# A four-layer graph network: the last three destination chunks of layer 3 summed over lists of fetched rows in place of dense products

## The chip, the cores and the metric

The kernel runs on one core of a Trainium2 chip. The metric is the device time of one execution in microseconds (us). TensorE (PE) multiplies matrices; VectorE (DVE), ScalarE (ACT) and GpSimd (POOL) do the rest of the arithmetic; GpSimd and SyncE (SP) also issue DMA transfers.

## The reference

Each of four layers replaces x by layernorm(x + layer(x, adj)). `adj` is a 2708 x 2708 symmetric matrix of zeros and ones with about 16 ones in a row; x has 512 columns.

```python
def _layernorm(x, axis=-1, eps=1e-5):
    m = jnp.mean(x, axis=axis, keepdims=True)
    v = jnp.var(x, axis=axis, keepdims=True)
    return (x - m) / jnp.sqrt(v + eps)
deg = jnp.maximum((adj != 0).astype(jnp.float32).sum(-1), 1.0)
# layer 0: dinv = rsqrt(deg); relu(((dinv * (adj + I) * dinv) @ x + x) @ W0 + b0)
# layer 1: ((dis[:, None] * adj * dis[None, :]) @ x) @ W1.T + b1, dis = (adj.sum(1) + 1e-8) ** -0.5
# layer 2: twice: proj = x @ W; Wh, Ws = split(proj); a = softmax(Wh @ Ws.T) * adj
#          x = leaky_relu(a @ Wh + x, 0.01)
# layer 3: adj @ (x @ W3) + b3   (8 heads side by side)
```

For layer 3 the kernel computes (adj @ x) @ W3 + b3, then adds x and normalises.

## The kernel before

**Tiles and stages.** The 2708 nodes are 22 blocks of 128 rows (the last has 20). Where a layer sums over neighbours, the *destinations* are cut into six chunks of columns (`CH`): 512, 512, 512, 512, 384 and 276. The *sources* are taken in six groups of blocks (`GROUPS`: 0-3, 4-7, 8-11, 12-15, 16-18, 19-21). A step of the dense form is one pair (chunk k, group g).

**Dense sums (layers 0, 1 and 3).** `prepare` (L782) casts the mask bytes `at` to 32-bit tiles `m` on ScalarE, and, at a layer's first chunk, `halve` (L713) splits the rows x of a source block into two halves: `xh` by ScalarE and `xl` = x - `xh` by VectorE. `multiply` (L849) then adds into four accumulators `acc[k][d]`, one for each 128 of the 512 columns of x, the products `xh` x `m` and `xl` x `m` for every source block. After the last group `evict` (L919) moves the accumulators to `ht`, `project` (L936) multiplies each block of 128 destinations by W (four fp32 products `mm`), `combine` (L976) adds the residual row `xres`, and `finish` (L995) calls `layernorm` (L634) and writes the rows out. `residual` (L964) fetches `xres` by a DMA that GpSimd issues. Block 21 has only 20 rows: its projection is spread over four partitions' quarters (`few`, L652), and the four parts are then added (`total`, L662).

**The masks in DRAM.** While layer 0 runs, the bytes of `adj` are kept in DRAM tiles `masks[k]` (128 x 22 x width of the chunk), which layers 1 to 3 read again as `at<-mask`, loads that SyncE issues.

**Lists.** During layer 1, `index` (L1097) and `one_hot` (L1221) build, for every destination block, lists of 128 row numbers (`givers`): four "rest" lists of sources that any of the block's 128 destinations may have as a neighbour, and eight quarter lists, two for each 32 destinations (block 21: three lists only). Every neighbour of the block is in one of its lists once.

**Attention (layer 2).** Class `Attention` (L1275) works through two graph attention layers. For each destination chunk it computes scores and softmax weights, writes rows of `pairs` (a projected row of 512 numbers with weights at either side) to DRAM, fetches 128 of these rows for one list by an indirect DMA on GpSimd (`fetch`, L1562, into one of eleven buffers `wide`), and adds to an accumulator with one fp32 product for a full list, whose stationary operand is the fetched weights (128 x 128) and whose moving operand is the fetched row, or with four products of 128 x 32 for one turn of quarter lists (`weigh`, L1609). The rows after the second attention layer are kept on chip for the next layer, and written to `saved[2]` in DRAM.

**What sets the order.** `Ordered` (L53) chains the instructions of every engine in the order in which the program issues them, so each engine's queue is in program order and every issue is recorded at L70; groups of instructions are told apart by their tiles' names. The program itself decides the order by a clock of estimated costs: `advance` moves it, `later` puts off a step until it has passed, and generators that yield are taken as fillers. At the end of layer 2 the filler is `early` (L598): layer 3's products for chunks 0 to 2 (`TWO` = 3) and groups 0 to 3, since the rows of these sources are ready first. Their partial sums are copied to pages `begun`. After the attention, `step` (L1043) does the remaining steps: groups 4 and 5 of chunks 0 to 2, then all six groups of chunks 3, 4 and 5, with the projections and layernorms of a chunk done by `ends` (L1079) between the steps of the next.

## Time and profile before

| | us |
|---|---|
| median of 3 runs (2367.58 to 2376.91) | 2368.28 |
| the profiled execution, its own time | 2338.2 |
| span of the profile | 2336.5 |
| PE busy | 2274.8 |
| DVE busy | 1474.8 |
| ACT busy | 662.2 |
| POOL busy | 762.3 |

The mean granted TensorE clock is 0.993 of full speed. The profiled execution is 30 us shorter than the median of the runs. In the profile a row such as "PE acc<-m,xh 128*128 128x512 f32 x1" names the engine, the output and input tiles, the size of the stationary operand and that of the output; a bracket at its end gives the idle time before it and what ended it. "PEld" is the loading of stationary operands. An entry of the chain of waits has its start, its duration, the engine and the output tile. In a table of stretches each column is an engine's busy time, then the granted clock, the share of the DMA engines and GB/s.

### The profile page before, as it was taken

Reading aid. Unit: us, or ns where it says so; the run is one execution under the profiler, and the core shown is the slowest. Engines: PE = TensorE matmul, PEld = TensorE weight load, DVE = VectorE, ACT = ScalarE, POOL = GpSimd, SP = SyncE. Lnnn points to the kernel's source line nnn. Section 1 sums busy time; section 2 is a strip of 40 time slices with the busy share of each in tenths; the row PEclk is TensorE's granted clock in tenths of the full one; section 3 lists DMA queues with packets and bytes.
Section 4 is the critical chain, followed back from the end, with each engine's and each line's share of the span. In section 5 each row is a group of like instructions: output and inputs, shape, how many; then the busy total and the mean of one; then the engine's idle time right before and its main releaser. Section 6 shows DMA issues by size and latency. Waiting matters only on the chain.

```text
span 2336.5 us, 26171 instructions
## 1 busy us (share of the span) xinstructions
PE 2274.8 (97%) x8518; PEld 1292.5 (55%) x8518; DVE 1474.8 (63%) x2831; ACT 662.2 (28%) x1334; POOL 762.3 (33%) x879
## 2 busy tenths in 40 slices
PE   8999999999999999999999999999999999999997
PEld 6677677778644444443456444444443456566585
DVE  6999986786655529657677511228677788724523
ACT  6544353223100113222223200113232334432211
POOL 6645641111000000636375550000636466551000
PEclk9999999999999999999999999999999999999998
DMA  9765652222434404869699996405869799983311
GB/s 343 258 199 169 182 172 86 74 86 70 171 146 167 154 0 143 278 229 311 204 324 350 302 388 232 152 0 163 279 217 314 233 316 329 305 279 96 123 48 43
DMA packets 312440, 463.50 MB, mean 198 GB/s; under 512 B 60162, under 2 KB 189706, under 8 KB 312292
## 3 DMA queue, kind: packets, MB, share of 16 engines
q1 hardware_dynamic: 252276, 240.81, 31.5%
q0 software_dynamic: 60016, 220.92, 27.1%
q8 instruction: 69, 1.13, 0.2%
q14 instruction: 79, 0.65, 0.1%
HBM read 307.75 MB, written 153.85 MB: 198 GB/s over the span
## 4 chain that ended last, share of the span: by engine, by line
PE 84%; DVE 7%; DMA 4%; issue 2%; ACT 1%; POOL 1%; SPq 0%; DVEq 0%; ACTq 0%; POOLq 0%
PE sp L70 32%; PE acc L70 29%; PE mm L70 9%; PE z L70 6%; PE wst L70 6%; DMA pairs<-s 1%; DMA at<-in_adj_t 1%; DVE st L70 1%; DMA at<-mask 1%; ACT m L70 1%; DVE s L70 1%; PE list L70 1%; PE mix L70 0%; POOL bytes L70 0%; PE tr_x2t L70 0%
## 5 line engine op out<-in xcount | busy, mean ns | idle before, releaser
L70 POOL DMA_INDIRECT g<-pairs,givers x510 | 516.2, 1012 | 897.0 <-DMA pairs<-s 537.4
L70 PE MATMUL sp<-xs,wst_sb 128*128 128x512 f32 (+3 forms) x2112 | 797.7, 544 | 0.0
L70 PEld LDWEIGHTS sp<-xs,wst_sb 128*128 128x128 f32 (+1 forms) x2112 | 380.0, 186 | 406.8 <-issue 321.9
L70 PE MATMUL acc<-m,xh 128*128 128x512 f32 (+4 forms) x1584 | 571.4, 382 | 13.6 <-ACT m L70 7.0
L70 PE MATMUL acc<-m,xl 128*128 128x512 f32 (+4 forms) x1584 | 553.2, 367 | 1.5 <-DVE xl L70 1.5
L70 PEld LDWEIGHTS acc<-m,xh 128*128 128x128 f32 (+1 forms) x1584 | 290.3, 189 | 81.4 <-issue 22.3
L70 PEld LDWEIGHTS acc<-m,xl 128*128 128x128 f32 (+1 forms) x1584 | 290.3, 189 | 48.1 <-issue 5.7
L70 ACT COPY s<-sp 128x512 f32<-128x512 f32 (+2 forms) x252 | 133.6, 531 | 482.1 <-PE sp L70 469.5
L70 PE MATMUL acc<-g 128*32 128x512 f32 (+1 forms) x1020 | 260.8, 605 | 0.9 <-DMA g<-pairs,givers 0.5
L70 DVE TENSOR_TENSOR top<-top,s 128x512 f32<-128x512 f32 (+5 forms) x240 | 149.6, 623 | 170.6 <-ACT s L70 169.1
L70 PE MATMUL mm<-w,ht 128*128 128x512 f32 (+1 forms) x528 | 222.6, 593 | 8.1 <-DVE ht L70 8.1
L70 ACT CAST m<-at 128x512 fp32r<-128x512 uint8 (+5 forms) x396 | 199.2, 567 | 80.0 <-DMA at<-mask 63.7
L70 ACT ACTIVATE s<-s 128x512 f32<-128x512 f32 (+3 forms) x264 | 150.7, 580 | 236.6 <-DVE s L70 236.3
L70 DVE TENSOR_TENSOR sum<-sum,s 128x512 f32<-128x512 f32 (+4 forms) x252 | 157.4, 625 | 23.9 <-ACT s L70 23.9
L70 DVE TENSOR_TENSOR s<-s,a 128x512 f32<-128x512 f32 (+3 forms) x264 | 165.9, 628 | 10.2 <-DMA a<-mask 1.2
L70 DVE TENSOR_TENSOR s<-s,shift 128x512 f32<-128x512 f32 (+3 forms) x264 | 162.8, 620 | 6.7 <-ACT shift L70 6.7
L70 PEld LDWEIGHTS mm<-w,ht 128*128 128x128 f32 (+1 forms) x528 | 95.5, 186 | 124.4 <-issue 110.9
L70 PE MATMUL wst<-xt,mixed 128*128 128x512 f32 (+2 forms) x384 | 152.5, 550 | 1.7 <-ACT mixed L70 1.7
L70 PEld LDWEIGHTS acc<-g 128*32 128x32 f32 (+1 forms) x1020 | 75.4, 134 | 136.9 <-issue 115.8
L70 PE MATMUL z<-w,xt 128*128 128x512 f32 (+1 forms) x352 | 151.0, 596 | 0.0
L70 DVE COPY z_sb<-z 128x512 f32<-128x512 f32 (+1 forms) x44 | 30.3, 690 | 179.5 <-PE z L70 176.3
L70 POOL DMA_DIRECT2D x<-o x44 | 26.0, 596 | 358.0 <-DVE o L70 354.2
(167 smaller groups left out, 1657.4 us busy)
## 6 DMA issues: line engine op xcount, KB each, us to landing
pairs<-s SPq DMA_DIRECT2D x378, 128.0 KB
pairs<-z_sb SPq DMA_DIRECT2D x84, 512.0 KB
at<-in_adj_t SPq DMA_DIRECT2D x84, 256.0 KB
xres<-x POOLq DMA_DIRECT2D x44, 256.0 KB, 4.3
x<-o POOLq DMA_DIRECT2D x43, 256.0 KB, 3.1
x<-x SPq DMA_DIRECT2D x37, 256.0 KB
at<-mask SPq DMA_DIRECT2D x32, 256.0 KB
xt<-t SPq DMA_DIRECT2D x32, 256.0 KB
```

The lines of the kernel that those rows point to most:

```text
L70: ins = call(*args, **kw)
```

## The change

Layer 3's chunks 3, 4 and 5 (destination blocks 12 to 21) no longer have dense products. Each destination block is summed over its lists instead, as in the attention, then turned, projected and normalised.

- *Rows with bytes at their sides.* A new DRAM tile `rows3` has one row of 3220 bytes for each node: 640 bytes of `adj` for blocks 12 to 16, the 2048 bytes of x, 532 bytes of `adj` for blocks 17 to 21. The rows of x that the attention writes (`saved[2]`) now go to its middle. `give`, called in layer 1 after the eviction of chunks 3, 4 and 5, copies the bytes there from `masks[k]`, DRAM to DRAM, in four copies that SyncE issues (512 bytes a piece for chunk 3, 128 and 256 for chunk 4, 276 for chunk 5; 2816 pieces each).
- *Lists.* The new class `Listed` gathers the rows (one indirect DMA a list on GpSimd, 111 in all; a row brings the bytes of its block and what lies between them and x), casts the bytes of its block to fp32 weights on ScalarE (one cast of 128 x 128 for a full list, four of 128 x 32 for a quarter turn; three buffers in turn, which used to be the `hit` and `both` buffers of the lists' building), and multiplies. Block 21 comes first, then 12 to 20. After a block's last list VectorE copies the sum to `sum3`, TensorE transposes it in four pieces, ScalarE copies these to `turned3`, and the projection follows. Two blocks are normalised together.
- *The layernorm of `Listed`* does its last step on ScalarE (`scalar=True`: Identity with a scale and a bias), with one more small step on VectorE for the bias.
- *Order.* Group 4 of chunk 2 moves to the end of `early`, into the attention. The rest of chunks 0 to 2, in half steps, and their projections (`rest`) are the fillers between the lists. They use one half of PSUM, the lists the other.
- *Smaller things.* The residual rows of layer 3 are loaded by SyncE instead of GpSimd. Block 21's four parts are added straight to its residual. The `wide` buffers grow from 640 to 672 fp32 columns. The `hit` tile has one buffer in place of two.

The diff, without unchanged surroundings and with the old body of the projection loop left out:

```diff
@@ -41,6 +41,12 @@
+LISTED = (3, 4, 5)
+FIRST, MIDDLE = 12, 17
+ASIDE = (MIDDLE - FIRST) * P
+ROW = 4 * D
@@ -118,8 +124,13 @@
-            for s in range(3)
+            for s in range(2)
+        self.rows3 = scratch.tile(
+            [NP, ASIDE + ROW + N - MIDDLE * P], U8, tag="rows3", name="rows3"
+        )
+        x = self.rows3[:, ASIDE : ASIDE + ROW].bitcast(FP)
+        self.saved.append([x[i * P : (i + 1) * P, :] for i in range(NB)])
@@ -523,7 +534,7 @@
-    def wide(self, name, shape=(P, D + P)):
+    def wide(self, name, shape=(P, D + ASIDE // 4)):
         return self.wides.tile(list(shape), FP, tag="wide", name=name)
@@ -556,18 +567,14 @@
-            run.seq += [(l3, k, g) for g in (4, 5) for k in range(2)]
-            run.seq += [(l3, k, g) for k in range(2, TWO) for g in (4, 5)]
-            run.seq += [(l3, k, g) for k in range(TWO, len(CH)) for g in range(len(GROUPS))]
+            run.seq.append((l3, TWO - 1, 4))
+            run.early = len(run.seq)
+            run.seq += [(l3, k, g) for k in range(TWO) for g in (4, 5) if g == 5 or k < TWO - 1]
-            for t in range(4 * TWO, len(run.seq)):
-                self.step(run, t)
-            ly, k = run.before
-            for i, n, ps in self.project(ly, k):
-                self.finish(ly, k, [(i, n, self.combine(ly, i, n, ps))])
+            listed = Listed(self, l3)
+            listed.run(self.rest(run, listed))
@@ -604,7 +611,7 @@
         yield True
-        for t in range(4 * TWO):
+        for t in range(run.early):
             ly, k, g = seq[t]
@@ -616,22 +623,47 @@
-            if g == 3:
+            last = g == (4 if k == TWO - 1 else 3)
+            if last:
-            for n, j in enumerate(range(*GROUPS[g])):
+            for n in range(DC):
-                    self.multiply(ly, k, g, [j])
+                    self.multiply(ly, k, g, [n])
-                if g == 3:
+                if last:
-    def layernorm(self, rows):
+    def rest(self, run, listed):
+        for t in range(run.early, len(run.seq)):
+            ly, k, g = run.seq[t]
+            self.before_products(run, t)
+            if (ly, k) != run.before:
+                self.residual(ly, k)
+                run.before = ly, k
+            for d in range(DC):
+                self.multiply(ly, k, g, ds=[d])
+                listed.advance(3 * 2 * 0.226)
+                if d % 2:
+                    yield True
+            if g == 4:
+                continue
+            self.evict(ly, k)
+            self.biased(ly, k)
+            yield True
+            for i, n, ps in self.project_blocks(ly, k):
+                listed.advance(DC * cost(D))
+                listed.later(2.0, lambda a=(i, n, ps): listed.end(*a))
+                yield True
+    def layernorm(self, rows, scalar=False):
@@ -644,6 +676,18 @@
+        if scalar:
+            shift = small.tile([P, DC], FP, tag="ln_shift", name="ln_shift")[:, :m]
+            nc.vector.scalar_tensor_tensor(shift, mv[:, :m, 0], -1.0, y, ALU.mult, ALU.mult)
+            for q, (r, o, n) in enumerate(rows):
+                nc.scalar.activation(
+                    o[:n],
+                    r[:n],
+                    AF.Identity,
+                    bias=shift[:n, q : q + 1],
+                    scale=y[:n, q : q + 1],
+                )
+            return
@@ -850,26 +894,28 @@
-        starts, stops = ((0, 16), (15, NB - 2)) if two else ((0,), (NB - 2,))
+        b = GROUPS[4 if k == TWO - 1 else 3][1]
+        starts, stops = ((0, b), (b - 1, NB - 2)) if two else ((0,), (NB - 2,))
-            half = 0 if two and blocks[0] == 0 else k
+            half = 0 if two else k
-            for x in (ly.hi, ly.lo):
+            for x in (ly.hi, ly.lo) if 0 in ds else ():
-                        start=False,
+                        start=(blocks[0] in starts and x is ly.hi),
+            starts = ()
@@ -935,37 +981,31 @@
...
+    def project_blocks(self, ly, k):
+        half = 0 if ly.number == 3 else k
...
         for i, lo, n in blocks_of(k):
+            yield i, n, self.times_w(ly, half, i, n, lambda c: ly.ht[k][c][:, lo : lo + n])
+    def times_w(self, ly, half, i, n, columns):
+        nc, name = self.nc, f"mm{ly.number}_{i}"
+        if n <= QW:
+            return self.few(half, name, n, D, columns, lambda c: ly.w[c])
+        ps = self.bank(half, name)
+        for c in range(DC):
+            nc.tensor.matmul(ps[:n], columns(c), ly.w[c], start=(c == 0), stop=(c == DC - 1))
+        return ps
-            t = self.page(f"xres{ly.number}_{i}")
-            self.nc.gpsimd.dma_start(t, ly.source[i])
-            ly.done["xres", i] = t
+            self.residual_of(ly, i)
+    def residual_of(self, ly, i):
+        t = self.page(f"xres{ly.number}_{i}")
+        (self.nc.sync if ly.number == 3 else self.nc.gpsimd).dma_start(t, ly.source[i])
+        ly.done["xres", i] = t
@@ -976,6 +1016,10 @@
         nc, x = self.nc, ly.done.pop(("xres", i))
+        if n <= QW and ly.number == 3:
+            for c in range(DC):
+                nc.vector.tensor_add(x[:n], x[:n], ps[c * QW : c * QW + n])
+            return x
         if n <= QW:
@@ -992,7 +1036,7 @@
-    def finish(self, ly, k, parts):
+    def finish(self, ly, k, parts, scalar=False):
@@ -1000,7 +1044,7 @@
             out.append((i, o, n))
-        self.layernorm([(x, o, n) for (_, n, x), (_, o, _) in zip(parts, out)])
+        self.layernorm([(x, o, n) for (_, n, x), (_, o, _) in zip(parts, out)], scalar)
         for i, o, n in out:
@@ -1072,6 +1116,8 @@
             run.before, run.phase = (ly, k), 0
+            if ly.number == 1 and k in LISTED:
+                self.attention.give(k)
             if ly.number == 1:
@@ -1231,8 +1277,10 @@
-        tile_ = lambda tag, w: self.lists.tile([P, NB, w], BF, tag=tag, name=f"{tag}{s}", bufs=2)
-        hit, both = tile_("hit", LISTS), tile_("both", 2 * LISTS)
+        tile_ = lambda tag, w, bufs: self.lists.tile(
+            [P, NB, w], BF, tag=tag, name=f"{tag}{s}", bufs=bufs
+        )
+        hit, both = tile_("hit", LISTS, 1), tile_("both", 2 * LISTS, 2)
@@ -1311,6 +1359,19 @@
+    def give(self, k):
+        for i0, i1 in ((FIRST, MIDDLE), (MIDDLE, NB)):
+            blocks = [b for b in blocks_of(k) if i0 <= b[0] < i1]
+            if not blocks:
+                continue
+            lo, width = blocks[0][1], sum(n for _, _, n in blocks)
+            at = (blocks[0][0] - i0) * P + (ASIDE + ROW if i0 == MIDDLE else 0)
+            self.nc.sync.dma_start(
+                self.k.rows3[:, at : at + width].rearrange("(j p) i -> p j i", p=P),
+                self.k.masks[k][:, :, lo : lo + width],
+            )
@@ -1778,6 +1839,140 @@
+class Listed:
+    AHEAD = WIDES - 1
+    def __init__(self, fast, ly):
+        self.f, self.k, self.nc, self.ly = fast, fast.k, fast.nc, ly
+        blocks = [b for k in LISTED for b in blocks_of(k)]
+        self.to_weigh = []
+        for i, _, n in [blocks[-1], *blocks[:-1]]:
+            ts = lists_of(i)
+            self.to_weigh += [(i, n, t, t is ts[0], t is ts[-1]) for t in ts]
+        self.to_fetch = [(i, t) for i, _, ts, _, _ in self.to_weigh for t in ts]
+        self.fetched, self.pending = [], []
+        self.clock, self.free = 0.0, 3.0
+        self.done, self.turns = [], 0
+    def advance(self, us):
+        self.clock += us
+        while self.pending and self.pending[0][0] <= self.clock:
+            self.pending.pop(0)[1]()
+    def later(self, us, what):
+        self.pending.append((self.clock + us, what))
+        self.pending.sort(key=lambda a: a[0])
+    def fetch_ahead(self):
+        while self.to_fetch and len(self.fetched) < self.AHEAD:
+            i, t = self.to_fetch.pop(0)
+            g = self.f.wide(f"g3_{i}_{t}")
+            if i < MIDDLE:
+                first, width = (i - FIRST) * P, (MIDDLE - i) * P + ROW
+            else:
+                first, width = ASIDE, ROW + (i - MIDDLE) * P + rows_of(i)
+            self.nc.gpsimd.indirect_dma_start(
+                out=g.bitcast(U8)[:, :width],
+                out_offset=None,
+                in_=self.k.rows3,
+                in_offset=bass.IndirectOffsetOnAxis(ap=self.k.givers[:, i, t : t + 1], axis=0),
+                element_offset=first,
+            )
+            self.free = max(self.free, self.clock) + 1.25
+            self.fetched.append((g, self.free + 5))
+    def weigh(self, wait=False):
+        nc, f = self.nc, self.f
+        self.fetch_ahead()
+        if not self.to_weigh:
+            return False
+        i, n, ts, first, last = self.to_weigh[0]
+        there = self.fetched[len(ts) - 1][1]
+        if there > self.clock:
+            if not wait:
+                return False
+            self.advance(there - self.clock)
+        self.to_weigh.pop(0)
+        gs = [self.fetched.pop(0)[0] for _ in ts]
+        if first:
+            self.acc = f.bank(1, f"acc3_{i}")
+            f.residual_of(self.ly, i)
+        side = len(ts) > 1
+        self.turns += 1
+        tag, bufs = ("both", 2) if self.turns % 3 else ("hit", 1)
+        weights = f.lists.tile([P, P], FP, tag=tag, name=f"weights3_{i}", bufs=bufs)
+        at, z = (0, (MIDDLE - i) * P // 4) if i < MIDDLE else (ROW + (i - MIDDLE) * P, 0)
+        for h, g in enumerate(gs):
+            lo, rows = (h * QW, QW) if side else (0, n)
+            nc.scalar.copy(
+                weights[:, lo : lo + rows], g.bitcast(U8)[:, at + lo : at + lo + rows]
+            )
+        for h, g in enumerate(gs):
+            lo, rows = (h * QW, QW) if side else (0, n)
+            nc.tensor.matmul(
+                self.acc[lo : lo + rows],
+                weights[:, lo : lo + rows],
+                g[:, z : z + D],
+                start=first,
+                stop=last,
+            )
+        self.advance(1.1 if side else cost(D))
+        if last:
+            self.later(1.5, lambda a=(i, n, self.acc): self.turn(*a))
+        self.fetch_ahead()
+        return True
+    def turn(self, i, n, acc):
+        nc, f = self.nc, self.f
+        r = f.page(f"sum3_{i}")
+        nc.vector.tensor_copy(r[:n], acc[:n])
+        def turn():
+            ps = f.bank(1, f"tr3_{i}", (P, DC, P))
+            for c in range(DC):
+                nc.tensor.transpose(
+                    ps[:, c, :n], r[:n, bass.ts(c, P)], self.k.ident[:n, :n]
+                )
+            t = f.page(f"turned3_{i}", FP, (P, DC, P))
+            nc.scalar.copy(t[:, :, :n], ps[:, :, :n])
+            self.advance(0.45)
+            self.later(1.2, lambda: self.project(i, n, t))
+        self.later(1.2, turn)
+    def project(self, i, n, t):
+        f, x = self.f, self.ly.done["xres", i]
+        ps = f.times_w(self.ly, 1, i, n, lambda c: t[:, c, :n])
+        self.nc.vector.tensor_add(x[:n], x[:n], self.ly.bt[:n])
+        self.advance((1 if n <= QW else DC) * cost(D))
+        self.later(2.0, lambda: self.end(i, n, ps))
+    def end(self, i, n, ps):
+        f = self.f
+        self.done.append((i, n, f.combine(self.ly, i, n, ps)))
+        if len(self.done) > 1 or not self.to_weigh:
+            f.finish(self.ly, None, self.done, True)
+            self.done = []
+    def run(self, products):
+        while True:
+            if self.weigh() or next(products, False):
+                continue
+            if self.pending:
+                self.advance(self.pending[0][0] - self.clock)
+            elif not self.weigh(True):
+                return
```

More of the change, by code (lines that the diff above doesn't have):

```diff
@@ L936, in project @@
     def project(self, ly, k):
-        nc = self.nc
-        parts = []
+        return list(self.project_blocks(ly, k))
+    def project_blocks(self, ly, k):
+        half = 0 if ly.number == 3 else k
         for i, lo, n in blocks_of(k):
-            if n <= QW:
-                ps = self.few(
-                    k,
-                    f"mm{ly.number}_{i}",
-                    n,
-                    D,
-                    lambda c: ly.ht[k][c][:, lo : lo + n],
-                    lambda c: ly.w[c],
-                )
-                parts.append((i, n, ps))
-                continue
-            ps = self.bank(k, f"mm{ly.number}_{i}")
-            for c in range(DC):
-                nc.tensor.matmul(
-                    ps[:n],
-                    ly.ht[k][c][:, lo : lo + n],
-                    ly.w[c],
-                    start=(c == 0),
-                    stop=(c == DC - 1),
-                )
-            parts.append((i, n, ps))
-        return parts
+            yield i, n, self.times_w(ly, half, i, n, lambda c: ly.ht[k][c][:, lo : lo + n])
[7 more added lines that the diff above has]
+        return ps
     def residual(self, ly, k):
         for i, _, _ in blocks_of(k):
-            t = self.page(f"xres{ly.number}_{i}")
-            self.nc.gpsimd.dma_start(t, ly.source[i])
-            ly.done["xres", i] = t
+            self.residual_of(ly, i)
[3 more added lines that the diff above has]
+        ly.done["xres", i] = t
     def biased(self, ly, k):
```

## The prediction

> **What bounds the kernel now.** I read the page from its first part down, then the stretches after the attention, the chain of waits there, and the order in time of the matrix and gather engines.
>
> The busy times say that TensorE sets the time almost everywhere:
>
> ```profile
> PE 2274.8 (97%) x8518; PEld 1292.5 (55%) x8518; DVE 1474.8 (63%) x2831; ACT 662.2 (28%) x1334; POOL 762.3 (33%) x879
> ```
>
> In the end of the span, where the change works, every other engine is nearly empty (columns: stretch and its length, busy time of PE, weight loads, DVE, ACT, POOL, granted clock, DMA share, GB/s):
>
> ```profile
> 2200.00:2240.00 40.00, 40.00 (x179) 31.62 (x178) 11.16 (x26) 11.62 (x25) 0.54 (x1) 1.00 0.21 63
> 2280.00:2320.00 40.00, 40.00 (x223) 29.00 (x221) 13.63 (x36) 6.61 (x21) 1.59 (x3) 1.00 0.15 46
> ```
>
> GpSimd and the DMA engines are free, so gathers could be taken in; TensorE work removed here is worth its full time as long as nothing makes TensorE wait. The chain that ended last has the pieces that go away:
>
> ```profile
> 2121.82 0.20 ACT rs_t L70
> 2122.02 0.48 ACT begun L70
> 2122.55 20.42 PE acc L70 x89
> ...
> 2178.78 11.78 PE acc L70 x54
> 2190.56 13.73 PE mm L70 x32
> 2204.29 37.31 PE acc L70 x176
> 2241.60 13.73 PE mm L70 x32
> 2255.34 28.38 PE acc L70 x176
> 2283.72 10.30 PE mm L70 x24
> 2294.02 18.10 PE acc L70 x144
> 2312.12 3.45 PE mm L70 x8
> ```
>
> The `acc` pieces from 2178.78 on are the dense products of layer 3's chunks 3 to 5 (the first also holds chunk 2's last group, 24 products, 4.3 us). A projection `mm` of one block is 3.43 us (13.73 / 4). Note the first two lines: TensorE stood still for 2.7 us because an eviction was queued on ScalarE behind a square root.
>
> What lists cost is seen in the attention, which already sums over lists. TensorE and then GpSimd, in order of time (start, duration):
>
> ```profile
> 2090.80 1.06 PE L70 MATMUL acc<-g 128*32 128x512 f32 x8
> 2091.79 0.50 PE L70 MATMUL acc<-m,xh 128*128 128x512 f32 x1
> 2100.31 1.88 PE L70 MATMUL acc<-g 128*128 128x512 f32 x4
> 2122.55 0.80 PE L70 MATMUL acc<-m,xh 128*128 128x512 f32 x1 [2.70 <-ACT begun L70]
> 2123.14 0.63 PE L70 MATMUL acc<-m,xl 128*128 128x512 f32 x1
> 2123.57 0.63 PE L70 MATMUL acc<-m,xh 128*128 128x512 f32 x1
> ```
>
> ```profile
> 2099.62 0.95 POOL L70 DMA_INDIRECT g<-pairs,givers  x1 [0.31 <-issue]
> 2100.87 0.94 POOL L70 DMA_INDIRECT g<-pairs,givers  x1 [0.30 <-issue]
> ```
>
> Two full lists take 1.72 us (0.86 each), a turn of four quarter lists 1.1, a gather is issued every 1.25, and its median landing is 5.9 us after issue. After the 2.7 us gap the products start 0.43 us apart instead of 0.2275.
>
> **The Trainium skill.** "TensorE: Matmul & The Clock Gate", Part 1, says that after an idle window of about 3.4 us the array runs at half clock. The 0.43 us pitch agrees, and here a 2.7 us gap was enough; gaps of 1.2 to 2.3 us elsewhere in this trace mostly cost nothing. "DMA: Bandwidth & Descriptors", section "How a descriptor splits into AXI transactions", says that a read that doesn't start on a 256 B boundary fetches from the boundary below. The new rows have a pitch of 3220 B, so nearly all gathers start off one; at about 128 B more on some 2400 this is an estimated 5%. No run here shows it yet.
>
> **The change part by part.** Times are of the profiled execution (span 2336.5 us).
>
> *Removed:* the dense products of chunks 3 to 5: 11.78 - 4.3 + 37.31 + 28.38 + 18.10 = 91.3 us.
>
> *Added on TensorE:* blocks 12 to 20 have 4 full lists and 2 quarter turns each, block 21 has 3 full lists: 39 x 0.86 + 18 x 1.1 = 53.3; ten sets of four transposes at about 0.44 (16 took 1.77 in layer 1), 4.4. Sum 57.7. Projections stay. Net -33.5 us.
>
> *Added on ScalarE:* per block 4 casts of 128x128 bytes at about 0.3 us (a 32x128 copy is 0.296) and 8 of 128x32 at about 0.2 (128x24 is 0.179), the copy of the turned sum 0.6, and now the last step of each layernorm 0.58: some 4 us per block, little as a sum. It matters as a queue, because each product now needs a cast first.
>
> *New waits.* I walked the built order of the five engines. For a typical block TensorE has: two full lists, a projection of chunks 0 to 2 (3.43), transposes of the block before, two full lists, its projection, quarter turn, a second chunk projection, quarter turn: 16.4 us. Two waits are in it:
> (a) Behind the transposes ScalarE copies the turned sum before it casts the next list: 0.2 + 0.6 + 0.3 + 0.05 = 1.15 us; nine times, with a shorter one for block 21, 10 us.
> (b) The last quarter turn's casts stand behind a pair's layernorm on ScalarE. From the end of that pair's last projection: 0.2, residual and statistics on DVE to the square root 2.65, back and five small steps to the shift 1.4, two normalisations 1.15, four casts 0.8, 0.1: 6.3 us. TensorE has 1.1 + 3.43 = 4.5 us of work meanwhile, so it waits 1.8. Five such waits of 1.7 to 2.6: 9.7 us. The first pair (blocks 0 and 21) is worse, since block 21's four partial adds run in series on DVE: 5.3 us, and 1.7 for half clock. The last blocks have no fillers left: two waits of 2.3 and 1.9.
> Sum of new waits: 10 + 9.7 + 7 + 4.2 = 31 us.
>
> *Moved:* group 4 of chunk 2 now closes the attention's interleaved part. Its halves `xh` and `xl` of blocks 16 to 18 are queued behind the last chunk's layernorm: DVE ends that at 2124.5 and needs 3 x 0.69 more, so TensorE waits from 2118.2 to about 2126.7 and then partly at half clock. It is ready for the lists at about 2142.1; before, the equal amount of work was done at 2138.6. +3.5 us. The 2.6 us wait for DVE near 2162 goes: -2.6.
>
> *Gathers:* 3 + 9 x 12 = 111. The rows land at about 2127, POOL is through at 2127 + 111 x 1.25 = 2266 if never held, well before TensorE needs the last. The first is needed at 2142 and lands near 2133. On the DMA engines the page's software queue moved 220.92 MB in 27.1% of the span, 349 GB/s; the largest gather, 344 KB, is 0.99 us, 1.04 with the extra bytes, under 1.25. Hidden, with 1.6 us per gather (19.2 / 12) as the limit.
>
> *Copies of mask bytes:* four, of 2816 pieces each. On SyncE 128 pieces take 0.44 us to issue, so one copy is 9.5 us, and the two of chunk 4 together 19. They delay layer 1's third mask load from 573.0 to about 585; its bytes are needed near 600.4, so 11 us are to spare. Taken as 0; if the pieces are twice as dear, some 8 us.
>
> *One `hit` buffer less:* DVE alone writes and reads it, in order: 0. *Residual loads on SyncE:* each stands behind `out` writes that wait on ScalarE, but is asked for a block or more ahead: 0.
>
> *End:* before, DVE works 8.8 us past the last matmul (block 21's adds); after, block 20's pair needs 5.3: -3.4.
>
> Sum: -33.5 + 31 + 3.5 - 2.6 - 3.4 = -5 us; my walk through the whole order gave -8, and I take -6. The runs shown have a median of 2368.28, 30 us above the profiled execution; the difference is carried over as it is: 2362.
>
> **Rivals.**
> *The waits are covered* (ScalarE runs further ahead than I think, shorter small steps): then -33.5 - 2.6 - 3.4 + 3.5 and some 8 us of waits (a), -28: 2340. For it: ScalarE is under 30% busy. Against: its queue is in order, and the first chain line above shows just such a queueing.
> *The gathers become the bound:* from 1.6 us each on it decides. At 1.8 us they end at 2127 + 200, then 26 us of landing, sum, turn, projection and layernorm: 2353, +16: 2384, slower. For it: rows off the boundary, eleven buffers freed in bursts. Against: the attention holds 1.25 us with rows nearly as long while other transfers run.
> *The copies hold up layer 1*, or something in the early part moves: +8 of cost on top of the forecast, 2370.
>
> **How the numbers follow.** The forecast has 0.47, covered waits 0.27, gathers 0.17, copies 0.09. About 0.5% (11.8 us) is what a measurement of this kernel can tell from no change. The forecast's own range is 2352 to 2372: 0.2 of it faster, nearly all the rest the same. Covered waits are faster nearly always; gathers are slower 7 times in 10; copies split between same and slower. Faster 0.39, same 0.41, slower 0.20. The range 2334 to 2386 reaches into both rivals.
>
> **What would show it.** Right: TensorE busy about 30 us less after 2142, with gaps before `acc<-g` of 1.1 us released by ScalarE after transposes and of 1.7 to 2.6 before the second quarter turn; the largest near 2157. GpSimd gathers at 1.25 us or held by TensorE. Wrong: gaps before `acc<-g` released by DMA (gathers), a gap in layer 1 near 600 released by a mask load (copies), or hardly any gaps and an end near 2308 (covered).

## The result, and the profile after

The changed kernel takes 2375.66 us (median of 20 runs), the kernel before, run beside it, 2372.14 us (20 runs). The ratio of the means is 1.0023 [1.0007, 1.0039]: 5.5 us slower (the medians lie 3.5 us apart), a small difference within the 0.5% that was called no change. The forecast was 2362, 6 us faster; the time lies in its range, but the change went the other way.

The profiled execution after has an own time of 2382.5 us and a span of 2380.8 us. The page, first part:

```profile
PE 2270.6 (95%) x8252; PEld 1237.8 (52%) x8252; DVE 1470.1 (62%) x2841; ACT 669.1 (28%) x1408; POOL 854.7 (36%) x968
```

TensorE has 266 matrix instructions fewer than before and GpSimd 89 instructions more, but TensorE's busy time fell by only 4 us. The same two stretches as before, by windows (columns as in the prediction):

```profile
2200.00:2240.00 40.00, 36.55 (x130) 17.45 (x130) 10.63 (x30) 11.98 (x39) 24.41 (x26) 0.97 0.80 262
2280.00:2320.00 40.00, 33.19 (x111) 14.26 (x110) 15.57 (x38) 8.07 (x32) 22.81 (x24) 0.96 0.76 241
```

Where TensorE had been busy all 40 us, it now stands still for 3.5 and 6.8 us, and the granted clock is no longer 1.00. The two profiled executions differ also outside the change, so the fair piece to compare is the tail: from the end of the attention's last sum to the end of the span. It is worked out from every matrix record:

| tail, us | length | TensorE busy | idle | after its last product |
|---|---|---|---|---|
| before, as profiled for the prediction | 220.0 | 198.3 | 5.6 | 16.2 |
| before, profiled again | 219.2 | 196.8 | 6.2 | 16.2 |
| after | 230.7 | 182.1 | 35.3 | 13.2 |

The waits, over TensorE's part of the tail, before (waiting engine and tile, releaser: us in total, times, longest):

```profile
PE acc L70 <- ACT begun L70: 2.7, 1, 2.7
PE mm L70 <- DVE ht L70: 2.6, 1, 2.6
```

and after:

```profile
PE acc L76 <- ACT weights L76: 14.5, 7, 4.2
PE mm L76 <- ACT turned L76: 4.5, 2, 3.8
PE acc L76 <- ACT xh L76: 4.1, 1, 4.1
PE acc L76 <- issue: 3.7, 5, 0.9
PE tr L76 <- DVE sum L76: 2.7, 2, 1.8
```

The largest entry is the one forecast: products that wait for their casts (`weights`) on ScalarE. The idle time grew by 29.7 us, where the prediction's new waits came to 31. What doesn't fit is the second column: 16 us less busy time, not 33. The granted clock was half for 30.7 us of TensorE's part of this tail, in five windows (3.4 us in one window before). TensorE was busy for 23.5 us of them, so some 12 us are lost there, against 1.7 before; the other 7 us were not traced apart. "TensorE: Matmul & The Clock Gate", Part 1, of the Trainium skill tells of half clock after an idle window of about 3.4 us; the trace agrees on the factor (0.5 in the record of the granted clock), but one 3.4 us stretch here, at 2352.6, came after two gaps of 1.8 and 1.9 us.

### The profile page after: what moved, and what is told of

Same layout as the page of the kernel before. It is cut to its first block, busy times and chain, and to the rows that moved or that the text cites. A ratio compares the mean times of both kernels' runs of the same rounds, so it can differ in the third digit from the quotient of the medians.

```text
span 2380.8 us, 26033 instructions
## 1 busy us (share of the span) xinstructions
PE 2270.6 (95%) x8252; PEld 1237.8 (52%) x8252; DVE 1470.1 (62%) x2841; ACT 669.1 (28%) x1408; POOL 854.7 (36%) x968
## 4 chain that ended last, share of the span: by engine, by line
PE 71%; issue 13%; DVE 8%; DMA 3%; POOL 3%; ACT 1%; another core or an unknown queue 1%; SPq 0%; POOLq 0%; ACTq 0%; DVEq 0%
PE sp L76 31%; PE acc L76 21%; PE z L76 6%; PE wst L76 6%; PE mm L76 5%; POOL g L76 1%; DVE st L76 1%; DMA at<-in_adj_t 1%; DMA t<-x2t 1%; DVE r L76 1%; DMA g<-pairs,givers 1%; DVE rs_t L76 1%; POOL x L76 0%; DMA g<-rows,givers 0%
## 5 line engine op out<-in xcount | busy, mean ns | idle before, releaser
L76 PE MATMUL acc<-m,xh 128*128 128x512 f32 (+3 forms) x1320 | 486.3, 389 | 14.5 <-ACT m L76 5.6
L76 PE MATMUL acc<-m,xl 128*128 128x512 f32 (+3 forms) x1320 | 470.1, 373 | 6.1 <-DVE xl L76 4.8
L76 PEld LDWEIGHTS acc<-m,xh 128*128 128x128 f32 (+1 forms) x1320 | 242.0, 189 | 79.7 <-issue 24.9
L76 PEld LDWEIGHTS acc<-m,xl 128*128 128x128 f32 (+1 forms) x1320 | 242.2, 190 | 49.9 <-issue 8.1
L76 PE MATMUL mm<-w,ht 128*128 128x512 f32 (+1 forms) x448 | 195.2, 602 | 5.4 <-DVE ht L76 5.4
L76 ACT CAST m<-at 128x512 fp32r<-128x512 uint8 (+5 forms) x330 | 170.4, 576 | 56.2 <-DMA at<-mask 39.0
L76 POOL DMA_INDIRECT g<-rows,givers x111 | 105.4, 949 | 106.2 <-PE acc L76 74.1
```

Source lines behind the costliest of these rows:

```text
L76: ins = call(*args, **kw)
```

## The experiments

The theory at the outset was that casts in ScalarE's queue cost what the prediction says, and that the moved group or the gathers cost the rest. Rivals: the moved group, the copies in layer 1, or the gathers by their bytes or their rate. All ratios are to the kernel before on the same chip, whose median was 2367 to 2370 us except where another is given.

**The kernel before, profiled again** (no edit).

> The kernel before, unchanged, for a second profile. Its first profiled execution took 2338.2 us, 34 under the median of its other runs; the changed kernel's profile has three stops in the attention (7.3 us at 1228, 5.2 at 1317, 5.2 at 1946) that the first profile of before lacks. If these belong to the execution and not to the change, this profile spans some 2365 to 2375 us and has such stops in the attention too, and its end (from the attention's last list product to the end of the span) stays near the 220 us of the first profile. If they belong to the change, it spans about 2338 and has none.

It took 2363.92 us (one run), 26 us more than the execution that the prediction was read from. Its tail is the same (table above). The difference is in the attention, where TensorE now stands still in a few places (waits of 900 to 2143 us):

```profile
PE tr_mx L70 <- issue: 4.8, 2, 4.2
PE tr_mx L70 <- DVE wide L70: 4.8, 6, 2.9
PE tr_top L70 <- issue: 2.8, 1, 2.8
```

In before's first profile the waits on `tr_mx` are at most 0.7 us each, and there is no such stop. In these places an engine that should copy TensorE's finished result starts late. Counting the copies that start over 0.5 us after TensorE's recorded end with their engine free: none in the first profile of before, 26 in this one (41 us in sum), 25 in after (67 us). I call these late signals below; they become the main point.

**Casts issued ahead.** The casts of the next two lists go to pages and are issued before the current list's products.

```diff
+CASTS = 2
+        weights = self.f.page(f"weights3_{i}", FP, (P, P))
...
+    def cast_ahead(self):
+        while len(self.ready) < min(CASTS, len(self.to_weigh)) and len(self.fetched) >= len(
+            self.to_weigh[len(self.ready)][2]
+        ):
+            if not self.cast():
+                return
```

> The changed kernel with the casts of the next two lists issued on ScalarE ahead of what follows, into pages, instead of right before their product. Theory A (ScalarE's queue: casts behind turned copies and layernorms hold TensorE): about 14 us of waits before list products go, and with them some half clock: 12 to 18 us less than the changed kernel, ratio to before about 0.996. Theory B (gathers land late and hold TensorE): the casts still wait for them, within 3 us of the changed kernel, ratio 1.001 to 1.004. Theory C (the moved group, and half clock after it): no more than 5 us less, ratio about 1.000.

1.0018 [1.0006, 1.0031]. In the profile the waits for `weights` fell from 14.5 to 10.2 us, but a projection waited 5.3 us for `ht` instead, and an unnamed wait ("issue") of 4.5 us came up. Being earlier in the program is not enough, and something else held TensorE.

**The moved group put back.**

```diff
-            run.seq.append((l3, TWO - 1, 4))
             run.early = len(run.seq)
-            run.seq += [(l3, k, g) for k in range(TWO) for g in (4, 5) if g == 5 or k < TWO - 1]
+            run.seq += [(l3, k, g) for k in range(TWO) for g in (4, 5)]
```

> The changed kernel with group 4 of chunk 2 taken out of the attention's interleaved part and put back among the products after it. Theory A: the wait behind the last layernorm shrinks from 5.9 us to the 2.7 of before and 1.7 to 3.4 us of half clock go, but the waits among the lists stay: 4 to 6 us less than the changed kernel, ratio about 1.000. Theory B: the first gathers start as late as before, no change, ratio 1.002. Theory C: 8 us less or more, ratio under 0.999.

1.0031 [1.0016, 1.0045], tail 229.6 us. The move isn't what made the change slower.

**Nothing of a list waited for.** Products read resident tiles; the gathers are issued, but nobody uses or frees their rows, so GpSimd runs free. No casts.

```diff
-            nc.scalar.copy(
-                weights[:, lo : lo + rows], g.bitcast(U8)[:, at + lo : at + lo + rows]
-            )
+        weights = self.k.ident
...
-                g[:, z : z + D],
+                self.ly.w[h],
```

> The changed kernel without the casts, with the list products on resident tiles (identity as weights, rows of W3 as moving operand): it leaves out the adjacency bytes and does not use the gathered rows, though it still gathers them. No list product waits for ScalarE or for a gather; transposes, projections and layernorms stay. Theory A or B: the waits before list products, 20 us in the profile of the changed kernel, go, and part of 15 us of half clock: 20 to 30 us less than the changed kernel, ratio about 0.990 to 0.994; against the casts issued ahead it tells how much of that the gathers hold. Theory C: no more than 8 us less.

1.0386 [1.0353, 1.0419], 2460 us: far from what was expected. TensorE stood still twice, for 69 and 36 us, while GpSimd issued its 111 gathers back to back. None of the theories held until then had a mechanism for it, and it set the next runs.

**Neither gathers nor casts; then casts without gathers.** The first is the last edit with the gathers gone too. The second keeps the casts, from a resident tile, in their places in ScalarE's queue.

```diff
-            self.nc.gpsimd.indirect_dma_start(
...
-                weights[:, lo : lo + rows], g.bitcast(U8)[:, at + lo : at + lo + rows]
+                weights[:, lo : lo + rows], self.k.ident.bitcast(U8)[:, lo : lo + rows]
```

> The changed kernel with its 111 gathers and their casts left out; the list products run on resident tiles (identity, rows of W3), so the adjacency bytes and the fetched rows are left out of layer 3's last chunks. All theories: the floor of the change, TensorE's work with only the turned copies, projections and layernorms around it. From the profile of the changed kernel: its end took 230.7 us from the last list product of the attention; less the 20 us before list products, 8 us of late copies and 8 to 12 us of half clock, 190 to 196, that is some 25 to 30 us under before, ratio 0.988 to 0.991.

> As the run without gathers and casts, but the casts are kept, in their places in ScalarE's queue, from a resident byte tile (the adjacency bytes and fetched rows are left out). Theory A (casts queued behind turned copies and layernorms on ScalarE eat the gain): 15 to 20 us more than the run without casts, ratio about 0.996. Theory D (the gathers eat it: while GpSimd issues them back to back, others see TensorE's semaphore microseconds late): within 8 us of the run without casts, ratio 0.992 or less, and the rest of the way to the changed kernel is the gathers'.

Without both: 0.9882 [0.9851, 0.9913], -28 us. With the casts: 0.9978 [0.9967, 0.999], -5 us. So the casts cost 23 us, and the gathers 10.7 more to the change's +5.5. (Two runs below, both with the casts issued ahead and both on one chip, put the gathers at 14 us: 1.0034 with, 0.9974 without.) The waits in the tail without both:

```profile
PE acc L76 <- ACT xh L76: 4.1, 1, 4.1
PE tr L76 <- DVE sum L76: 2.5, 2, 1.7
PE acc L76 <- DVE xl L76: 2.1, 1, 2.1
PE mm L76 <- ACT turned L76: 0.7, 1, 0.7
```

and with casts alone:

```profile
PE acc L76 <- ACT weights L76: 15.8, 13, 4.2
PE acc L76 <- ACT xh L76: 4.1, 1, 4.1
```

The tail of casts alone is 213.7 us (busy 175.3, idle 25.3), of neither 190.9 (busy 167.8, idle 9.6). The thirteen waits for `weights` are the whole difference in idle time between these two; of the 7.5 us more of busy time, half clock explains about 4.

**Which gaps the gathers add.** Going through TensorE's gaps of after and of casts alone, product by product, most are the same to 0.02 us (4.20 for the first pair, 1.70, several of 0.87 and 1.05). Three are much longer, and all three follow a late signal. The largest, by the order in time on TensorE:

```profile
2247.47 0.60 PE L76 MATMUL tr<-ident,sum 128*128 128x128 f32 x4
2247.90 3.60 PE L76 MATMUL mm<-w,ht 128*128 128x512 f32 x8
2255.31 1.22 PE L76 MATMUL mm<-w,turned 128*128 128x512 f32 x1 [3.81 <-ACT turned L76]
```

ScalarE:

```profile
2245.30 0.50 ACT L76 CAST weights<-g 128x128 f32<-128x128 uint8 x2 [7.42 <-PE acc L76]
2254.67 0.58 ACT L76 COPY turned<-tr 128x512 f32<-128x512 f32 x1 [8.88 <-remote]
```

and GpSimd:

```profile
2249.46 0.95 POOL L76 DMA_INDIRECT g<-rows,givers  x1 [0.30 <-issue]
2250.71 0.94 POOL L76 DMA_INDIRECT g<-rows,givers  x1 [0.30 <-issue]
2252.75 0.94 POOL L76 DMA_INDIRECT g<-rows,givers  x1 [1.10 <-remote]
```

The transposes end at 2248.07; ScalarE is idle from 2245.8, yet its copy of them starts at 2254.67, 6.6 us late, just after a run of gathers 1.25 us apart is over. The same happens near 2293.6 and 2313.4. The three add 3.81, 1.33 and 2.61 us of standing still. Two smaller ones add 0.77 (at 2245.6, cause not traced) and 0.96 (at 2352.7, behind a copy that starts 0.85 us late). Three windows of half clock follow the first, the third and the last, and TensorE is busy for 11.9 us in them, some 6 us lost. Together this is 15.4 of the 17.0 us by which these two tails differ (230.7 against 213.7; by their ratios the kernels differ by 10.7). The tails without gathers (before in both profiles, neither, casts alone, and the later ones) have no late signal at all.

"Perfetto Trace Analysis", "Per-instruction lifecycle", says that a matmul's end in the profile is an estimate and its semaphore goes out and spreads later. The trace agrees, and narrows down what was late, since it also records the updates of semaphores. TensorE's update for these transposes is recorded at 2254.65, 6.6 us behind their end (in before's first profile the median is 0.014 us) and 0.02 us ahead of the copy, though TensorE had begun the next products at 2247.90. So ScalarE started as soon as the update was there, and the update came late.

**Fewer gathers ahead.** `AHEAD` is 6 in place of 10, to shorten the runs.

```diff
-    AHEAD = WIDES - 1
+    AHEAD = 6
```

> The changed kernel with at most 6 list rows fetched ahead instead of 10, so that GpSimd issues its gathers in shorter bursts. Theory D: the late copies after bursts of 8 and more gathers (6.6, 1.6 and 2.7 us of ScalarE's waiting in the profile of the changed kernel) go, with their half clock: 6 to 12 us less than the changed kernel, ratio 0.997 to 1.000. If gathers were late by landing, fewer in flight make it worse: 3 to 10 us more, ratio 1.004 to 1.007, with waits of list products for gathers. Theory A alone: no change, 1.002.

1.015 [1.0123, 1.0177], inconclusive: the program's own clock took lists as not yet landed and spent the fillers early, so the last 100 us had lists only, and runs of 16 gathers still occurred.

**Narrow gathers.** Nothing waited for, as above, but each gather brings only 512 bytes a row.

```diff
-                out=g.bitcast(U8)[:, :width],
+                out=g.bitcast(U8)[:, :512],
...
-                element_offset=first,
+                element_offset=ASIDE,
```

> As the run without list waits (products on resident tiles, gathers free to run; bytes and rows left out), but each gather fetches 512 bytes of a row instead of some 2,600. That run stood still twice, 69 and 36 us, with a VectorE copy waiting for TensorE's finished sum while GpSimd issued 111 gathers without a pause. If the bytes on the DMA engines did it, the stops go and the time is some 2340 to 2350; if the issuing itself did it, they stay, and the time is again above 2430.

2468.95 us (one run), with stops of 77 and 34 us, the first behind a copy that starts 75.3 us late. A fraction of the bytes, much the same stops: not bytes.

**Four kernels on one chip on which before takes 2341.55 us.** No late signal of over 0.5 us shows anywhere in the profiles taken there, not even in the attention, whose gathers are unchanged, so nothing on that chip could tell how to avoid them. The traces bear a second mark of the difference. In these four, and in the first profile of before, TensorE's semaphore updates are all recorded but one at most. In the fifteen others all are there up to the attention's first gather, and over the whole execution 14 to 17% are missing (in after, 1391 of 1676 are recorded).

> As the run with casts from a resident byte tile and no gathers (ratio 0.9978), but the casts of the next two lists are issued ahead, into pages. If the 23 us that the casts cost over the floor (0.9882) are their place in ScalarE's queue, most go: ratio 0.989 to 0.992. If they are the casts' own time or something else of ScalarE, the ratio stays at 0.996 to 0.998.

Casts ahead, no gathers: 0.9966 [0.9955, 0.9976], tail 212.2 us, idle 24.6. So without gathers, too, casting ahead gains next to nothing (casts alone had 213.7).

Nothing waited for, with three (short) or eight (long) small `memset` on GpSimd after each gather:

```diff
+            rest = self.f.lists.tile([P, 32], BF, tag="rest", name=f"pause3_{i}_{t}", bufs=1)
+            for _ in range(3):
+                self.nc.gpsimd.memset(rest, 0.0)
```

> As the run without list waits (products on resident tiles, 111 gathers free to run; bytes and rows left out; 2460 us), but GpSimd does three tiny memsets, an estimated 0.35 us, after each gather. If the stops come of gathers issued back to back, even such a pause lets TensorE's signals through: 2340 to 2355 us. If they come of the number of gathers or of their landing, the stops stay: above 2430.

> The same with eight memsets, about 1 us, after each gather. If back-to-back issue does it: 2340 to 2355 us, whatever the short pause gave. If only the number of gathers counts: above 2430.

> The changed kernel with three tiny memsets on GpSimd after each gather: one gather every 1.6 us at most, 178 us for 111, ending near 2340 in its profile's time against 2352 now. If back-to-back issue delays TensorE's signals and the pause cures it, the 8 us of late copies and their half clock go: 6 to 10 us less than the changed kernel, ratio 0.998 to 1.000. If not cured, or if gathers then land late, 1.002 or more.

2333.65 and 2427.92 us (one run each). The long pause sets the time by itself: gathers 2.51 us apart, the last at 2415.7, TensorE done at 2298.3. The third, the changed kernel with the short pause, took 1.0197 [1.0176, 1.0218]: its gathers come 2.04 us apart without waiting for buffers (1.6 in the kernel that waits for nothing; why the same pause costs more here was not found). That is the rival of the gather rate in pure form: +47 us, where the prediction's formula gives 2127 + 111 x 2.04 + 26 = 2379, +43 on a span of 2336.5.

**Where the casts wait.** Casts two ahead, and the layernorm of a pair put off as a whole by 4 us of the program's clock, with and without gathers.

```diff
-            f.finish(self.ly, None, self.done, True)
-            self.done = []
+            done, self.done = self.done, []
+            self.later(4.0, lambda: f.finish(self.ly, None, done, True))
```

> The changed kernel with the casts of the next two lists issued ahead, and each pair's layernorm in the list stage issued 4 us of the planner's clock later, so that ScalarE's square root and normalisation no longer stand before casts while they wait for VectorE. If ScalarE's order was the cause, 10 us or more go beyond the casts ahead alone (ratio 1.0018): 0.990 to 0.997. If the gathers then become what the lists wait for, 0.999 to 1.002.

> The same without gathers, casts and products from resident tiles (bytes and rows left out). If ScalarE's order was the cause of the casts' 23 us, it comes near the floor of 0.988: 0.986 to 0.991. If not, it stays at 0.996 to 0.998 as with casts ahead alone.

1.0034 [1.0019, 1.0048] and 0.9974 [0.9957, 0.999]: nothing gained. The wait had only moved: the statistics on VectorE came later too, so ScalarE's square root waited with all that was queued behind it (ScalarE, no gathers):

```profile
2223.18 0.20 ACT L77 ACTIVATE rs_t<-rs_v 128x2 f32<-128x2 f32 x1 [8.14 <-DVE rs_v L77]
2224.66 1.52 ACT L77 ACTIVATE o<-xres,ln_shift,y 128x512 f32<-128x512 f32 x2 [1.28 <-DVE ln_shift L77]
```

**Back to back or with a pause.** The kernel that waits for nothing, and the same with the short pause, on one chip (before 2367.5 us).

> The free gathers once more (products on resident tiles; bytes and rows left out), as the control of the next run. On a chip where the kernel before takes some 2370 us: two long stops again, above 2430. On one where it takes some 2340: no stops, 2310 to 2320.

> The free gathers with a short pause of GpSimd after each (bytes and rows left out), on the same chip as the control. If back-to-back issue makes TensorE's signals late: no stops where the control has them, under 2365. If the pause does not matter: as the control, above 2430.

2464.29 and 2350.1 us (one run each). Back to back (gathers 1.25 us apart), VectorE's copy of block 21's sum, what stands behind it, and TensorE's next product:

```profile
2242.71 0.68 DVE L76 COPY sum<-acc 20x512 f32<-20x512 f32 x1 [79.46 <-issue]
2243.32 1.86 DVE L76 TENSOR_TENSOR ht<-acc,begun 128x512 f32<-128x512 f32 x3
2244.04 5.57 PE L76 MATMUL mm<-w,ht 128*128 128x512 f32 x8 [70.11 <-issue]
```

and with 0.5 us of `memset` behind each gather (1.6 us apart):

```profile
2170.55 0.68 DVE L76 COPY sum<-acc 20x512 f32<-20x512 f32 x1 [8.20 <-PE acc L76]
```

In the first, TensorE's last product of the sum ends at 2173.93 and the copy starts 68.8 us later (the 79.46 is all of VectorE's idle time before it); TensorE's next product needs `ht`, which stands behind the copy in VectorE's queue. One small thing changed, and 114 us are gone. Gathers issued back to back make other engines see TensorE's finished work late; that is shown, on this chip, and the stops without a pause came on two other chips too (2460 and 2468.95 us). The pause makes the gathers both broken up and less frequent, and which of the two helps was not separated.

**ScalarE's steps of the layernorm apart.** Statistics at once; the square root 1.5 us and the last step 2 us later on the program's clock, casts two ahead, no gathers; then the same with the gathers, and the short pause after every fourth.

```diff
-            f.finish(self.ly, None, self.done, True)
+            mv, v = self.stats([(x, n) for _, n, x in done])
+            self.later(1.5, lambda: self.root(done, mv, v))
...
+        self.later(2.0, lambda: self.last(parts, y, shift))
```

> Casts ahead, no gathers (casts and products from resident tiles; bytes and rows left out), with the layernorm's statistics issued on VectorE at once, and ScalarE's square root 1.5 us and its last step 3.5 us of the planner's clock later. If the casts' place in ScalarE's queue costs the 23 us, no wait of 2 us or more before list products is left in the trace, and the ratio is 0.986 to 0.991. If the ratio stays at 0.996 to 0.998, the casts cost by something else.

> The same order of ScalarE's work with the gathers, and three tiny memsets on GpSimd after every fourth gather (an estimated 1.45 us per gather, 161 us in all). If both causes are as argued, the floor of 0.988 and a part of the gathers' 11 us: 0.989 to 0.995, faster than both kernels. If the late signals stay or gathers land late: 0.998 to 1.003.

Without gathers: 0.9887 [0.9854, 0.992], the floor again within the noise (tail 195.2 us, 190.9 without casts), though all the casts are there. Waits in its tail:

```profile
PE acc L77 <- ACT xh L77: 4.1, 1, 4.1
PE acc L77 <- ACT weights L77: 4.1, 4, 2.3
```

So the casts' 23 us are not work but their place in ScalarE's queue, behind steps that wait for VectorE. Taking away the order alone, with the casts kept, takes away the cost.

With gathers and pauses: 0.9958 [0.9945, 0.9971], 2356.65 us, about 10 us faster than before and 15 faster than the change. Late signals are smaller but not gone: the latest copies in its list stage start 1.54 and 1.12 us late (6.61 in after). It is still some 14 us above the same kernel without gathers, and part of that may now be the rate: of the products whose gather is issued from about 2296 us on, many start only 4.2 to 6.3 us after it, while in the changed kernel none starts less than 8.6 us after. How the 14 us divide between that and the shorter delays wasn't separated.

## Why the prediction was right or wrong

- **Removed and added on TensorE: right.** With waits nearly gone (the kernel with steps apart, no gathers), list products and transposes are busy for 54.1 + 4.5 = 58.6 us; 57.7 was worked out. With neither casts nor gathers the kernel is 28 us faster, which is the covered-waits rival's number.
- **New waits: the right mechanism and places, the sizes too high.** They stand where the walk through the queues put them. Waits (a), behind the turned copy, are 0.5 to 1.0 us and 5.8 in sum with casts alone (10 forecast); waits (b), before the second quarter turn, are one of 1.70 and four near 1.0, 5.8 in sum (9.7); the first pair is 4.2 (5.3), the last blocks 3.3 (4.2).
- **Half clock: mis-sized.** One loss of 1.7 us was in the sum of the waits, and part of the moved group's 3.5. With casts alone TensorE is already busy for 12.4 us at half clock, a loss of 6.2; in after for 23.5, a loss of 12. Smaller waits plus more half clock come out near the forecast: casts without gathers measure -5 us, the forecast's sum. That is luck: two errors offset each other.
- **"Gathers ... Hidden": the step that failed.** What it says of rate and bytes held: 84 of 110 gathers follow within 1.35 us, the first at 2161.8 and the last at 2351.9 because buffers hold them, and no product waits long for one. But the step put the gathers at nothing once they land in time, and they cost 10.7 us all the same, by a road that it didn't have: TensorE's signals arrive late during runs of gathers, and half clock follows. This turned -5 into +5.5. That gathers cost this is measured by taking them away; that the late signals are how is read from the gaps of one pair of profiles, which account for most of it. The rival "gathers become the bound" had the right suspect and the wrong reason; its rate limit is real (2.04 us: +47) but wasn't reached.
- **The 30 us carried over: a warning not read.** Before's profile lacked the late signals entirely, and its second profile, 26 us longer, has them in the attention, the one stage that gathers. The prediction carried the difference over as a constant, when it shows in the one stage that already has the kind of instruction that the change adds to the tail. That first execution looks like those of the chip without late signals: it took 2338.2 us, where before takes 2338.88 to 2347.21 us there, and its semaphore records are complete. So the forecast most likely joined a profile of one kind of chip to a median of another; the record does not say where that profile was taken. That the attention's stops have the same cause as those in the tail was not tried apart.
- **The moved group: a little undersized.** The waits for `xh` and `xl` came as described (4.11 and 1.77 us), with 10.2 us at half clock, in which TensorE is busy for 6.9; against before's 2.70, 2.62 and 3.4 us this is about +2, not +0.9. Putting the group back gained nothing, so this is no lever.
- **Copies of mask bytes, `hit`, residual loads: right at 0.** The first attention product after layer 1 starts at 787.55 us against 786.33, but in the second profile of before at 787.34.
- **The end: right.** 2.9 us shorter (3.4).

What the prediction named as signs came true in the main: gaps before `acc<-g` released by ScalarE, that of the first pair (forecast as the largest, near 2157) ending at 2197.7. The attention ends 33.7 us later here, so this is 2164 on before's scale. Its signs of error (gaps released by DMA, a gap near 600) did not appear, because the real error had another releaser: an engine waiting for TensorE.

Not tried: rows of a pitch that starts on a boundary, since nothing waited for the gathers' bytes; the changed kernel itself on the chip without late signals; the changed kernel with its gathers broken up but not made rarer; and whether recording the trace has a part in the late signals, since records are missing in just the executions that have them.

## What to carry to other kernels

When a cast is put between a fetch and a product, the cost is not its duration but what it stands behind: some 4 us of ScalarE work a block cost 23 us here, and went away when the steps that wait for another engine were issued later. A chain of gathers can cost time with neither its bytes nor its rate as the limit, so check how late the engines that read TensorE's results start while GpSimd issues. And where a profile is much shorter than the median, find out in which stage, and whether both come from the same chip, before carrying the difference over.

## What the runs showed of the hardware

Indirect gathers issued back to back, 1.25 us apart, delayed other engines' sight of TensorE's finished work by up to 68.8 us, and half a microsecond of other GpSimd work behind each took that away (2464.29 against 2350.1 us). Rows of 512 bytes did the same as long ones (2468.95 us, 75.3 us late at most). The recorded updates of TensorE's semaphore came late, not the waiting engines' starts behind them (2254.65 and 2254.67). ScalarE's and VectorE's own signals were not late: in the traces of after and of the gathers back to back, no instruction on TensorE, ScalarE or VectorE that waited for ScalarE or VectorE alone started over 0.5 us after the end it waited for. One chip showed none of this in four profiles: the kernel with the short pause took 2333.65 us there, and before 2341.55 instead of 2367.5. What in the machine holds the signal back stays open.
